# Adding the gated results to the token tiles by accumulating transfers of GpSimd instead of VectorE

## The chip, the core and the metric

The kernel runs on one core of a Trainium2 chip. A core has five engines that run side by side and meet at semaphores: TensorE (PE) multiplies matrices into eight banks of PSUM, VectorE (DVE) and ScalarE (ACT) work on tiles in SBUF and PSUM, GpSimd (POOL) computes in SBUF and issues transfers, and SyncE (SP) issues transfers. The transfers of all of them are carried out by the core's 16 DMA engines. The metric is the time of one execution on the device in microseconds (us); before the change it is 453.1 us, the median of three runs (452.22 to 453.49).

## The reference

The input x has 32 sequences of 128 tokens with 512 features in float32. Cut to what matters, each sequence goes through two residual halves:

```python
m = mask[:, :, None]
shift, scale, gate_msa = jnp.split(silu(t) @ ada_w + ada_b, 3, axis=1)
norm = jnp.where(m, layernorm(x) * (1 + scale[:, None]) + shift[:, None], 0.0)
ssm_out = jnp.where(m, mlp_fwd(norm) + mlp_bwd(norm), 0.0)   # exact gelu
x = x + gate_msa[:, None] * ssm_out
shift, scale, gate_mlp = jnp.split(silu(t) @ ffada_w + ffada_b, 3, axis=1)
ff_norm = layernorm(x) * (1 + scale[:, None]) + shift[:, None]
h = gelu(ff_norm @ ff_w1 + ff_b1, approximate=True)          # 512 -> 1024
return x + gate_mlp[:, None] * (h @ ff_w2 + ff_b2)           # 1024 -> 512
```

The first half counts only where the mask is set, which is a small part of the tokens. The second half is done for all 4096 tokens and is most of the work. The last line, `x + gate * result`, is what the change touches.

## The kernel before, in words

The opening (about the first 68 us) gathers the masked tokens into 512 slots, runs the first half on them, and leaves their new rows in a DRAM tensor, `x1_rows`. The rest is a loop over four **pairs**. A pair is two **sides** of four sequences each, so 1024 tokens; its tokens lie in four tiles x of 128 x 2 x 512, two for each side. Eight such tiles exist in the pool, so two pairs' tokens are in SBUF at a time, and the tokens of the pair after the next can only be loaded into a tile once its finished tokens have been stored.

Both matrix products of a pair are done by a scheme with seven block products in place of eight (P1 to P7), the first one nested twice. The **first product** (`FirstProduct`) works in streams 1, 2, 5, 6, 3, 7, 4; each stream has two banks, called e and a, and seven phases. Streams 5, 6, 7 and 4 read weight sums `tw` that are loaded from DRAM (`load_weights`, line 1069). Between the phases other engines alter the banks: `seed` (DVE, line 1167), the sum after P6 (DVE, line 1148, which needs a sum that POOL makes at line 1174), the sums after P7 and P4 (DVE, lines 1153 and 1158). PE then goes on in the same bank.

The **second product** (`SecondProduct`) runs over two column halves U and V in the order P1U P5U P1V P5V P2U P6U P2V P6V P3U P7U P3V P7V P4U P4V. Whenever a quarter of the output is complete in its bank, `finish` multiplies it by the gate into a tile t of 128 x 512 (line 1284; four buffers) and adds t to one half of the features of a token tile x (line 1286). There are eight such finishes in a pair. When both halves of a token tile are done, `store` (line 1290) sends the tile to the output, 512 KB, from SP's queue. While the second product of a pair runs, the tokens of the next pair are normalised, turned by small SBUF transfers into xT (line 961), scaled (ACT, line 944) and summed (DVE, line 991), and the first streams of its first product are put between the last steps (P4U and P4V).

All order is written out by hand: each engine gets its instructions in the order of the program, and every queue is in order. On SP's queue, at the end of a pair, there stand in a row the stores of the first two token tiles, the weights tw of stream 5, the loads of two token tiles of the pair after the next (line 412), the stores of the other two tiles, the weights tw of stream 6, and the loads of the last two tiles. On POOL's queue, after the sums of a first product, there stand the two gate loads of 1 MB each (line 901), and then the sums of the next first product (line 1174), mixed with gathers (line 890) that overwrite the rows of masked tokens in the newly loaded token tiles; a gather waits for the load of its tile. The last pair loads no tokens and gathers none.

Of the kernel before, what the change touches and what calls it, by code (L numbers as in the profile page):

```python
# [14 lines left out]
ALU = mybir.AluOpType  # L15
# [7 lines left out]
def kernel(  # L23
# [49 lines left out]
    nc = tc.nc  # L73
# [4 lines left out]
    NP = B // (2 * G)  # L78
# [99 lines left out]
    def group_of_tiles(name):  # L178
        return xnp.tile([P, G, D], F32, tag="xn", name=f"xn_{name}")
# [35 lines left out]
    def project(i, h, w, name, between=None, bank=(ps_o, "o"), seeded=None):  # L215

        pool, tag = bank
        po = seeded or pool.tile([P, 512], F32, tag=tag, name=f"po_{name}_{i}")
        for f in range(HC):
            if between and f in between:  # L220
                between[f]()
            nc.tensor.matmul(  # L222
                po,
                h[f][:, ts(i, P)],
                w[:, f, :],
                start=(f == 0 and seeded is None),
                stop=(f == HC - 1),
                skip_group_check=seeded is not None,
            )
        return po  # L230
# [6 lines left out]
    def gated(po, bias, gate, name):  # L237

        t = tp.tile([P, D], F32, tag="t", name=f"t_{name}")
        nc.vector.tensor_tensor(t, po, bias, ALU.add)  # L240
        nc.vector.tensor_tensor(t, t, gate, ALU.mult)
        return t
# [476 lines left out]
    def in_blocks(t):  # L719
        return t.rearrange("p g (h f) -> p (g h) f", f=2 * P)  # L720
# [59 lines left out]
    for f in range(KC):  # L780
        hidden_of_tile(f, 1)
        for done in (f - 1, f) if f % 2 else ():
            t = ssm.tile([P, NH], F32, tag="h", name=f"h_s0_{done}", bufs=HC)
# [28 lines left out]
    t = in_blocks(group_of_tiles("tw_3"))  # L812
# [418 lines left out]
    class SecondProduct:  # L1231
# [46 lines left out]
        def finish(self, c, side, h, result):  # L1278

            part = slice(h * D // 2, (h + 1) * D // 2)  # L1280
            view = result.rearrange("p (i d) -> p i d", i=2)
            t = tp.tile([P, 2, D // 2], F32, tag="t", name=f"t_o{self.p}_{c}_{side}{h}")
            gate = self.gate[side][:, 2 * c : 2 * c + 2, part]
            nc.vector.tensor_tensor(t, view, gate, ALU.mult)
            xt = self.xs[side][c][:, :, part]
            nc.vector.tensor_tensor(xt, xt, t, ALU.add)

        def store(self, c, side):
            b = (2 * self.p + side) * G + 2 * c
# [299 lines left out]
    with tc.If(more > 0):  # L1589
# [11 lines left out]
        with tc.For_i(0, more, 1):  # L1601
# [12 lines left out]
            for half_no, (mod, was, wbs, bias, bcol, func) in enumerate(  # L1614
# [25 lines left out]
                t = gated(project(0, h_l, wb, f"l{half_no}"), bias, gate_l, f"l{half_no}")  # L1640
# [59 lines left out]
```

## Time and profile before

| | before |
|---|---|
| median of three runs | 453.1 us (452.22 to 453.49) |
| profiled execution, span from the first to the last instruction | 451.7 us |
| part of the median that lies outside this span | 1.4 us |
| PE busy | 444.0 us (98%) |
| DVE busy | 334.5 us (74%) |
| ACT busy | 177.9 us (39%) |
| POOL busy | 158.4 us (35%) |
| granted TensorE clock | 1.000 |
| bytes moved by transfers | 70.84 MB, mean 157 GB/s |

The profiled execution is known by its span; the time of a run is longer by what lies around the span. Busy times are sums over one execution. Rows of a timeline give the start of an instruction from the beginning of the span, its duration, the engine, the line of the kernel, what it writes and reads, and in brackets the idle time of the engine before it with what ended that idle time. A queue's own rows carry a q (SPq, POOLq). An issue of a transfer is over long before the transfer has landed; landing times are in a list of their own.

### The profile page before, as it was taken

The page shows a single profiled execution, that of the slowest core. Times are in us where ns is not written, and L with a number is a line of the kernel's source. Part 1 is how long each engine was busy: PE and PEld are TensorE (multiplying, and loading weights), DVE is VectorE, ACT ScalarE, POOL GpSimd, SP SyncE. Part 2 cuts the span into 40 slices and gives each one's busy share as a digit, 9 for nine tenths or more (in the row PEclk, how much of TensorE's full clock was granted, in tenths as well). Part 3 has the DMA queues.
Part 4 walks back from the last instruction along what each step waited for, and adds up shares of the span by engine and source line. Part 5 has one row for each costly group of instructions (what it writes and reads, how often), then busy time and mean ns, then how long its engine had stood idle before and what let it go on. Part 6 is the DMA issues. An engine that isn't in the chain of part 4 may idle for free.

```text
span 451.7 us, 6204 instructions
## 1 busy us (share of the span) xinstructions
PE 444.0 (98%) x2147; PEld 370.2 (82%) x2147; DVE 334.5 (74%) x573; ACT 177.9 (39%) x389; POOL 158.4 (35%) x154
## 2 busy tenths in 40 slices
PE   8999999999999999999999999999999999999995
PEld 3884675688888888888888888888888888888884
DVE  5797788877799759977895689878956885434645
ACT  3123116353651551536526415464265244642000
POOL 4211470089770000897600007977000027560000
PEclk9999999999999999999999999999999999999999
DMA  6999449857327717741396177512971534122022
GB/s 250 372 399 408 177 65 308 284 187 229 129 97 168 108 49 268 235 138 36 105 177 93 46 267 230 141 38 86 189 99 47 176 128 129 35 93 95 0 94 96
DMA packets 85440, 70.84 MB, mean 157 GB/s; under 512 B 63396, under 2 KB 64508, under 8 KB 84382
## 3 DMA queue, kind: packets, MB, share of 16 engines
q1 hardware_dynamic: 64270, 57.76, 42.3%
q0 software_dynamic: 4160, 10.54, 6.9%
q10 hardware_dynamic: 16976, 2.11, 3.9%
q8 instruction: 18, 0.29, 0.3%
q14 instruction: 16, 0.13, 0.1%
HBM read 56.71 MB, written 13.70 MB: 156 GB/s over the span
## 4 chain that ended last, share of the span: by engine, by line
PE 84%; DMA 8%; DVE 3%; issue 2%; POOL 1%; SPq 0%; POOLq 0%
PE a_o L1310 24%; PE a_m L1123 21%; PE e_o L1310 18%; PE e_m L1123 16%; DMA fw<-in_L_cond_ff_w_dram 3%; PE po_s L222 3%; DMA w<-in_L_cond_bwd_w_dram 3%; DMA x_wide<-t_s 2%; DMA x<-x_wide,slot_i 1%; DVE t L403 1%; PE last L1310 1%; PE a_m_alone L1123 1%; POOL x L819 1%; PE ptr L950 0%; PE pl_s L255 0%
## 5 line engine op out<-in xcount | busy, mean ns | idle before, releaser
L1174 POOL TENSOR_TENSOR ha<-p_m,ha 128x512 f32<-128x512 f32 x20 | 25.8, 1292 | 176.0 <-ACT ha L1181 166.1
L1310 PE MATMUL e_o<-fw,ha 128*128 128x256 f32 x256 | 57.9, 379 | 0.0
L944 ACT ACTIVATE xT<-xT,modT 128x128 f32<-128x128 f32 x112 | 44.0, 480 | 28.1 <-DMA xT<-xn 28.1
L1310 PE MATMUL a_o<-t,hb 128*128 128x256 f32 x240 | 54.1, 379 | 0.0
L1310 PEld LDWEIGHTS e_o<-fw,ha 128*128 128x128 f32 x256 | 48.6, 190 | 6.6
L1310 PEld LDWEIGHTS a_o<-t,hb 128*128 128x128 f32 x240 | 45.6, 190 | 6.2
L1085 ACT ACTIVATE hb<-hb,biasT 128x256 f32<-128x256 f32 x64 | 29.0, 500 | 28.3 <-POOL hb L1207 16.1
L1137 ACT COPY p_m<-e_m 128x512 f32<-128x512 f32 x27 | 15.8, 586 | 51.6 <-PE e_m L1123 51.6
L890 POOL DMA_INDIRECT x<-x_rows,slot_i x24 | 27.2, 1135 | 6.2 <-issue 5.4
L1174 POOL TENSOR_TENSOR hb<-p_m,hb 128x512 f32<-128x512 f32 x20 | 29.2, 1460 | 0.3
L1310 PE MATMUL a_o<-fw,ha 128*128 128x256 f32 x128 | 28.9, 379 | 0.0
L1310 PE MATMUL a_o<-t,s 128*128 128x256 f32 x128 | 28.9, 379 | 0.0
L1310 PE MATMUL e_o<-fw,s 128*128 128x256 f32 x128 | 28.9, 379 | 0.0
L222 PE MATMUL po_s<-w,h_s 128*128 128x512 f32 x64 | 28.4, 594 | 0.0
L1181 ACT COPY ha<-e_m 128x512 f32<-128x512 f32 x32 | 18.5, 579 | 24.8 <-PE e_m L1123 24.4
L1310 PEld LDWEIGHTS a_o<-fw,ha 128*128 128x128 f32 x128 | 24.3, 190 | 3.3
L1310 PEld LDWEIGHTS a_o<-t,s 128*128 128x128 f32 x128 | 24.3, 190 | 3.3
L1310 PEld LDWEIGHTS e_o<-fw,s 128*128 128x128 f32 x128 | 24.3, 190 | 3.3
L1148 DVE TENSOR_TENSOR e_m<-a_m,ha 128x512 f32<-128x512 f32 x20 | 14.0, 698 | 17.0 <-POOL ha L1174 7.6
L1085 ACT ACTIVATE ha<-e_m,biasT 128x256 f32<-128x256 f32 x48 | 20.0, 468 | 14.4 <-PE e_m L1123 14.4
L1123 PE MATMUL a_m<-xT,tw 128*128 128x256 f32 x96 | 24.7, 380 | 0.0
L1123 PE MATMUL e_m<-s,fw 128*128 128x256 f32 x92 | 23.7, 380 | 0.0
(234 smaller groups left out, 894.1 us busy)
## 6 DMA issues: line engine op xcount, KB each, us to landing
x<-in_x_dram SPq DMA_DIRECT2D x16, 512.0 KB, 5.9
tw<-t_rows SPq DMA_DIRECT2D x16, 512.0 KB, 4.3
gate<-gate_rows POOLq DMA_DIRECT2D x8, 1024.0 KB, 5.1
out_dram<-x SPq DMA_DIRECT2D x15, 512.0 KB, 4.7
tw<-t_rows SPq DMA_DIRECT2D x16, 384.0 KB, 3.9
xT<-xn SPq DMA_DIRECT2D x80, 64.0 KB, 2.7
ada_f<-in_L_cond_ffada_w_dram SPq DMA_DIRECT2D x4, 768.0 KB, 14.8
ada_a<-in_L_cond_ada_w_dram SPq DMA_DIRECT2D x4, 512.0 KB, 3.6
```

Of the source, the lines that this page charges most:

```text
L222: nc.tensor.matmul(po, h[f][:, ts(i, P)], w[:, f, :], start=(f == 0 and seeded is None), stop=(f == HC - 1), skip_group_check=seeded is no ...
L403: engine.tensor_tensor(out, x, y, ALU.subtract)
L819: nc.gpsimd.indirect_dma_start(out=raw[i // 2][:, i % 2], out_offset=None, in_=x1_wide[:slots], in_offset=bass.IndirectOffsetOnAxis(ap=slo ...
L890: nc.gpsimd.indirect_dma_start(out=xs[i // G][i % G // 2][:, i % 2], out_offset=None, in_=x1_rows, in_offset=bass.IndirectOffsetOnAxis(ap= ...
L944: nc.scalar.activation(out, src, AF.Identity, bias=shift, scale=scale)
L1085: nc.scalar.activation(dst[:, n], src[:, n], AF.Gelu_apprx_tanh, bias=biasT[:, f : f + 1])
L1123: nc.tensor.matmul(bank[:, ts(n, QT)], self.w_block(j, product)[:, ts(n, P)], self.x_block(j, product), start=(product in ("P1", "P5") and ...
L1137: nc.scalar.copy(p5, e)
L1148: nc.vector.tensor_tensor(e, a, p5, add)
L1174: nc.gpsimd.tensor_tensor(self.place(RESULT[j], c), self.p5[j], other, ALU.add)
L1181: nc.scalar.copy(self.place(RESULT[j], c), src)
L1310: nc.tensor.matmul(part, src[:, k, ts(i, P)], w[product][:, k, :], start=(last and k == 0), stop=True, skip_group_check=True,)
```

## The change

In the first three pairs the addition at line 1286 is no longer an instruction of DVE. GpSimd issues a transfer from t to the same half of the token tile x, from SBUF to SBUF, that adds what it brings to what lies there; a partition's row of 512 values goes into two pieces of 256 values. The last pair keeps the addition on DVE. Everything else stays as written.

```diff
             gate = self.gate[side][:, 2 * c : 2 * c + 2, part]
             nc.vector.tensor_tensor(t, view, gate, ALU.mult)
             xt = self.xs[side][c][:, :, part]
-            nc.vector.tensor_tensor(xt, xt, t, ALU.add)
+            if self.p + 1 < NP:
+                nc.gpsimd.dma_start(xt, t, accum_op=ALU.add)
+            else:
+                nc.vector.tensor_tensor(xt, xt, t, ALU.add)
```

24 rows leave DVE and 24 come to POOL; line numbers behind the change grow by three. On POOL, at the end of the first pair, between the gate loads and the first sums of the second pair's first product (x_205 to x_208 are the four token tiles of the pair, t_o_0 and t_o_1 the gated results of U and V):

```order
 L901 DMA gate_0_1193<-gate_rows 128x2048
 L901 DMA gate_1_1237<-gate_rows 128x2048
+L1287 DMA x_205<-t_o_0_00_1303 128x2x256
+L1287 DMA x_206<-t_o_1_00_1358 128x2x256
+L1287 DMA x_205<-t_o_0_01_1389 128x2x256
+L1287 DMA x_207<-t_o_0_11_1414 128x2x256
+L1287 DMA x_206<-t_o_1_01_1427 128x2x256
+L1287 DMA x_208<-t_o_1_11_1447 128x2x256
+L1287 DMA x_207<-t_o_0_10_1474 128x2x256
+L1287 DMA x_208<-t_o_1_10_1494 128x2x256
 L1174 TENSOR_TENSOR ha_1432<-p_m_2_1514,ha_1432 128x2x256
 L1174 TENSOR_TENSOR hb_1433<-p_m_2_1514,hb_1433 128x2x256
```

Where POOL had nothing between the gate loads and the next pair's sums, eight issues now stand in the order of DVE's multiplications, and each waits for its own.

On DVE, the last finishes of the first pair (s, xT and sx are the blocks of the next pair's tokens):

```order
 L1284 TENSOR_TENSOR t_o_1_01_1427<-e_o_1_1212,gate_0_1193 128x512
-L1286 TENSOR_TENSOR x_206<-x_206,t_o_1_01_1427 128x2x256
 L991 TENSOR_TENSOR s_1_1402<-xT_0_1248,s_1_1401 128x1024
-L1340 TENSOR_TENSOR c_o_1_1445<-a_o_1_1213,p_o_1_1287 128x512
+L1343 TENSOR_TENSOR c_o_1_1445<-a_o_1_1213,p_o_1_1287 128x512
 L1284 TENSOR_TENSOR t_o_1_11_1447<-c_o_1_1445,gate_1_1237 128x512
-L1286 TENSOR_TENSOR x_208<-x_208,t_o_1_11_1447 128x2x256
 L1051 TENSOR_TENSOR sx_1459<-s_1_1401 128x512
 L1051 TENSOR_TENSOR sx_1459<-xT_0_1248 128x512
 L1284 TENSOR_TENSOR t_o_0_10_1474<-a_o_0_1155,gate_1_1237 128x512
-L1286 TENSOR_TENSOR x_207<-x_207,t_o_0_10_1474 128x2x256
 L1051 TENSOR_TENSOR sx_1459<-xT_1_1315 128x512
```

The additions are gone, and what stood behind them has moved up; the multiplications stay where they were.

On SP the rows and their order are the same, and only what the stores wait for is new. The last store of the first pair and the rows behind it, before:

```order
L1290 DMA out_dram<-x_208 128x2x512 [waits DMASW3_49,DMAHW4_49,DMASW2_49,DVE_49]
L1069 DMA tw_1_1498<-t_rows 128x1024 [waits DMASW1_49]
L1069 DMA tw_1_1498<-t_rows 128x768
L412 DMA x_1501<-in_x_dram 128x2x512 [waits DMAHW7_49,DMAHW3_49]
L412 DMA x_1503<-in_x_dram 128x2x512 [waits DMAHW4_49,DMAHW0_49]
```

and now:

```order
L1293 DMA out_dram<-x_208 128x2x512 [waits DMAHW4_49,DMASW7_49,DMASW1_49]
L1069 DMA tw_1_1498<-t_rows 128x1024 [waits DVE_49]
L1069 DMA tw_1_1498<-t_rows 128x768
L412 DMA x_1501<-in_x_dram 128x2x512 [waits DMAHW7_49,DMAHW3_49]
L412 DMA x_1503<-in_x_dram 128x2x512 [waits DMAHW4_49,DMAHW0_49]
```

The store waited for DVE's addition; it now waits for transfers that GpSimd issued (the DMASW semaphores). The wait for DVE has moved to the weights behind it, whose buffer is the one that DVE's multiplications read the gate from. The weights and the token loads still stand behind it.

## The prediction

> **What bounds the kernel now.** I read the page first: engine shares and the chain of waits.
>
> ```profile
> PE 444.0 (98%) x2147; PEld 370.2 (82%) x2147; DVE 334.5 (74%) x573; ACT 177.9 (39%) x389; POOL 158.4 (35%) x154
> PE 84%; DMA 8%; DVE 3%; issue 2%; POOL 1%; SPq 0%; POOLq 0%
> ```
>
> TensorE (PE) is busy for 444.0 of 451.7 us. Whether the rest lies where the change acts is told by the busy times by stretch, cut at the three places where one pair gives way to the next (columns: PE, weight loads, DVE, ACT, POOL, granted clock, DMA share, GB/s).
>
> ```profile
> 0.00:68.00 68.00, 65.04 (x423) 44.67 (x424) 52.25 (x144) 17.39 (x38) 25.37 (x44) 1.00 0.79 278
> 159.00:250.00 91.00, 91.00 (x422) 79.55 (x421) 71.28 (x108) 43.19 (x97) 36.07 (x30) 1.00 0.53 137
> 250.00:341.00 91.00, 91.00 (x422) 79.57 (x421) 71.37 (x108) 41.07 (x92) 36.06 (x30) 1.00 0.54 136
> ```
>
> From 159 to 341 us PE has no idle time at a full clock, and the waits of the opening are over before the first changed instruction (145 us). What PE still loses shows only in the chain, as a group of eight matmuls that takes longer than the usual 1.73:
>
> ```profile
> 199.53 0.86 PE e_m L1123 x4
> 200.39 1.97 PE a_m L1123 x8
> 202.36 0.86 PE e_m L1123 x4
> ```
>
> That is 0.24 us per pair. So relief for VectorE (DVE) has next to nothing to win; the question is which waits the change brings near PE.
>
> **What it removes.** The groups of DVE:
>
> ```profile
> L1286 DVE TENSOR_TENSOR x<-x,t_o 128x512 f32<-128x512 f32 x32 | 22.2, 692 | 1.1
> ```
>
> 24 of the 32 go, 24 x 0.692 = 16.6 us of DVE. All of it lies under matmuls, so I book 0 us. The cover is PE's own work, and it stays.
>
> **What it adds on GpSimd (POOL).** Eight transfers of 256 KB per pair stand in POOL's queue behind the two gate loads and ahead of the first sum of the next pair. POOL's timeline:
>
> ```profile
> 133.34 0.55 POOL L901 DMA_DIRECT2D gate<-gate_rows  x1 [1.45 <-PE a_m L1123]
> 181.22 1.26 POOL L1174 TENSOR_TENSOR ha<-p_m,ha 128x512 f32<-128x512 f32 x1 [47.34 <-ACT ha L1181]
> 190.06 1.23 POOL L890 DMA_INDIRECT x<-x_rows,slot_i  x1 [0.30 <-issue]
> 191.60 1.50 POOL L890 DMA_INDIRECT x<-x_rows,slot_i  x1 [0.30 <-ACT p_m L1137]
> 193.12 1.28 POOL L1174 TENSOR_TENSOR ha<-p_m,ha 128x512 f32<-128x512 f32 x1
> ```
>
> POOL is idle for 47.34 us just where they stand. No accumulating transfer is in the trace, so its issue is bounded by 0.55 us (gate, 128 rows) and 1.50 us (slowest gather); two pieces per partition make me take 1.1 us. The first seven end long before 181.22. The eighth waits for the last multiplication of DVE:
>
> ```profile
> 164.16 1.23 DVE L991 TENSOR_TENSOR s<-xT 128x1024 f32<-128x1024 f32 x1 [5.50 <-ACT xT L944]
> 169.63 0.68 DVE L1284 TENSOR_TENSOR t_o<-e_o,gate 128x512 f32<-128x512 f32 x1
> 178.21 0.68 DVE L1284 TENSOR_TENSOR t_o<-a_o,gate 128x512 f32<-128x512 f32 x1
> 178.93 0.69 DVE L1286 TENSOR_TENSOR x<-x,t_o 128x512 f32<-128x512 f32 x1
> ```
>
> The multiplication ends at 178.21 + 0.68 = 178.89; its issue is through at 180.0, 180.4 at the most, before 181.22. POOL pays nothing there: 0 us.
>
> **What it delays.** The store of a token tile now waits for the landing of a transfer in place of an addition of 0.69 us. Let L be the time from the end of the multiplication to the landing. Behind the stores on SP's queue, in order, stand the next weights (tw) and the tokens of the pair after (x):
>
> ```profile
> 171.07 0.38 SPq L1290 DMA_DIRECT2D out_dram<-x  x1
> 176.79 3.25 SPq L1290 DMA_DIRECT2D out_dram<-x  x2
> 180.09 1.34 SPq L1069 DMA_DIRECT2D tw<-t_rows  x2
> 181.52 1.95 SPq L412 DMA_DIRECT2D x<-in_x_dram  x2
> ```
>
> The last store goes at 176.79 + 3.25 - 0.38 = 179.66, 0.77 after 178.89. So it, and everything behind it, moves by D = L - 0.77. What that meets, by the landing times of the issue list (last column) and of the gathers:
>
> ```profile
> gate<-gate_rows POOLq DMA_DIRECT2D x8, 1024.0 KB, 5.1
> x<-in_x_dram SPq DMA_DIRECT2D x16, 512.0 KB, 5.9
> tw<-t_rows SPq DMA_DIRECT2D x16, 512.0 KB, 4.3
> ...
> DMA to landing us min/median/max: 2.5/3.1/5.4
> ```
>
> and by the readers, on PE and DVE:
>
> ```profile
> 167.41 1.03 PE L1123 MATMUL e_m<-s,fw 128*128 128x256 f32 x4
> 189.85 1.03 PE L1123 MATMUL e_m<-xn_sy,tw 128*128 128x256 f32 x4
> 197.64 1.03 PE L1123 MATMUL e_m<-xn_sy,tw 128*128 128x256 f32 x4
> 196.10 0.70 DVE L1148 TENSOR_TENSOR e_m<-a_m,ha 128x512 f32<-128x512 f32 x1
> ```
>
> Weights: issued at 180.09, landed at 184.39, read by PE at 189.85. They bear D = 5.46, so L = 6.2 us.
>
> Gathers: the x load issued at 181.52 lands at 187.42; the gather that writes into its tile is POOL's at 190.06, which leaves 2.64. If that gather waits, the sum L1174 behind it, which ends at 193.12 + 1.28 = 194.40, is late. DVE's L1148 needs it and must end by 197.64, where PE reads the bank: 197.64 - 0.70 - 194.40 = 2.54 more. Together D = 5.18, so L = 5.9 us. This case exists at two of the three places, since the third has no pair left to load. There only the weights count:
>
> ```profile
> 361.31 0.39 SPq L1290 DMA_DIRECT2D out_dram<-x  x1
> 361.80 0.41 SPq L1069 DMA_DIRECT2D tw<-t_rows  x1
> 371.75 1.03 PE L1123 MATMUL e_m<-xn_sy,tw 128*128 128x256 f32 x4
> ```
>
> 361.80 + 4.3 = 366.10 against 371.75: D = 5.65, L = 6.4 us. I take the second place as equal to the first.
>
> **How long is L?** Through GpSimd's queue a gather lands in 3.1 us and the gate's 1024 KB in 5.1. In between, 256 KB come to 3.1 + 2.0 x 256/1024 = 3.6 us on a quiet chip. The rings are not quiet where the last four of a pair run:
>
> ```profile
> 139.00:157.00 18.00, 18.00 (x85) 15.86 (x84) 15.59 (x21) 7.43 (x18) 0.00 (x0) 1.00 0.80 111
> 171.00:187.00 16.00, 16.00 (x76) 14.05 (x75) 15.21 (x23) 4.74 (x10) 5.30 (x4) 1.00 0.94 321
> ```
>
> From 171 to 187 us they are busy for 0.94 of the time. Gathers range up to 5.4, 2.3 over their median; I add half of that, 1.1, so L = 4.7 us. Bounds: not under the shortest gather, 2.5; not over the gate's 1024 KB plus the 2.3 of a crowded ring plus a second 0.55 of issue for the doubled pieces, 8.0. I stay near the low end since the bytes are a quarter of the gate's. At 4.7, 5.9 is not reached and nothing is paid.
>
> One rule speaks against the change. The Trainium skill (Collectives: The Full Stack, The bandwidth ceiling) says that an add in a transfer needs two source reads, which halved the measured bandwidth. By it the 256 KB would count as 512 and L would be an estimated 5.2 instead of 4.7; the sum would be the same, with less to spare. No run so far shows it.
>
> The four buffers of t are now freed by the landing, no longer by DVE's addition, so DVE's multiplications wait for transfers. The tile written at 169.63 comes round again some 8 us later, at 178.21; an L below that holds nobody up. Above it the next phase's sums for PE's banks, which stand behind on DVE, would be late.
>
> **Sum.** 0 (DVE) + 0 (POOL's issues) + 0 (stores, weights and gathers within their slack), and 0.2 us for POOL and DVE sharing the stretch after 181 us in another alignment, the size of the one stall seen. The profiled span is 451.7 us; the median of the runs, 453.1, lies 1.4 above it, which I carry along. Forecast: 453.3 us, no change. What a measurement here can tell from no change is about 0.3%, 1.4 us.
>
> **Rivals.**
>
> *Late landings make it slower.* From L = 5.9 us on, gather and sum on POOL, and a little later the weights, reach PE. For it: 0.94 DMA share, an unknown operation, two in-order queues behind it. Against it: rows of transfers with four times the bytes land in 5.1. At L = 8.0: (8.0 - 5.9) x 2 + (8.0 - 6.4) = 5.8 us, so 459 us. Over 1.4 us needs L above 6.4. Chance 0.33.
>
> *The turned blocks are held up.* From 139 to 157 us the small xT pieces keep the rings busy for 0.80; 18 x 0.20 = 3.6 us are free. Two transfers fall into it. At 321 GB/s one takes 0.8 us, with both operands read 1.6, both together 3.3 us: hidden. DVE's L991 ends at 164.16 + 1.23 = 165.39 and PE reads its result at 167.41, 2.0 us of slack. It would need twice that price, 6.6: 6.6 - 3.6 - 2.0 = 1.0 us at three places, 456 us. Chance 0.08.
>
> *DVE's relief shows.* Without the additions the 0.24 us at each of three places may go, and as much again elsewhere in a pair: 3 x 0.48 = 1.4 us, 451.7 us. Against it: PE shows no other gap. Chance 0.05. A smaller gain is part of the forecast.
>
> **How the numbers follow.** No change 0.54, the two slower cases 0.33 + 0.08 = 0.41, faster 0.05; the same three numbers are the chances of within 0.3%, slower and faster. The forecast's own range is 452.2 to 454.5. The range for 8 in 10 takes in L up to the bound with a little of both slower cases together: 452.0 to 460.0.
>
> **What would show it.** Right: PE still without idle time from 159 to 341 us; the store at 179.66 moves by some 4 us; the gather at 190.06 moves by less than 2.6 us; 24 fewer rows at the addition's line. Wrong: a PE group ended by DMA tw at about 190 us or by DVE L1148 at about 198 us, or gaps near 167 us behind ACT's scaling of xT. A landing of an accumulating transfer over 6 us would break the forecast; under 4 us it would make every slower case void.

## The result and the profile after

The changed kernel takes 470.2 us (median of four runs, 469.72 to 471.59) beside 452.7 us for the kernel before (four runs here, 452.22 to 453.49): 1.0385 times as long, 95% interval 1.0363 to 1.0407. No change was forecast, with 460.0 us as the upper end of the range. Its profiled execution took 469.7 us with a span of 468.0, 16.3 us more than the span of before. In all that follows one execution counts as slow, 470.8 us of a kernel whose other three took 458.3 to 463.9; it is left out of that kernel's ratio, and its trace is not used.

The busy times of the page, and the two stretches between pairs that were free of idle PE time before (columns as in the prediction: PE, weight loads, DVE, ACT, POOL, granted clock, DMA share, GB/s):

```profile
PE 451.3 (96%) x2147; PEld 374.5 (80%) x2147; DVE 318.5 (68%) x549; ACT 178.0 (38%) x389; POOL 185.9 (40%) x178
```

```profile
159.00:250.00 91.00, 86.38 (x384) 74.42 (x383) 62.34 (x96) 38.06 (x83) 43.50 (x37) 0.96 0.62 151
250.00:341.00 91.00, 85.90 (x385) 74.49 (x385) 61.18 (x96) 38.05 (x83) 43.57 (x37) 0.96 0.62 149
```

DVE is 16.0 us lighter, near the 16.6 that the prediction booked, and POOL heavier by 27.5. PE, which had no idle time here, now lacks 4.6 and 5.1 us in the two stretches, and its clock is no longer whole. PE's timeline at the end of the first pair and of the second says where (in brackets the idle time before and what ended it):

```profile
168.26 1.13 PE L1123 MATMUL e_m<-s,fw 128*128 128x256 f32 x4 [0.81 <-DVE s L991]
...
194.66 2.04 PE L1123 MATMUL e_m<-xn_sy,tw 128*128 128x256 f32 x4 [3.69 <-DMA tw<-t_rows]
196.50 1.91 PE L1123 MATMUL a_m<-xn_sy,tw 128*128 128x256 f32 x4
198.21 1.91 PE L1123 MATMUL e_m<-sx,tw 128*128 128x256 f32 x4
199.92 1.50 PE L1123 MATMUL a_m<-sx,tw 128*128 128x256 f32 x4
201.25 1.03 PE L1123 MATMUL e_m<-xn_sy,tw 128*128 128x256 f32 x4
...
294.16 2.05 PE L1123 MATMUL e_m<-xn_sy,tw 128*128 128x256 f32 x4 [5.10 <-DMA tw<-t_rows]
```

Three losses stand in these rows. PE waits 3.69 and 5.10 us for the next weights. Behind each wait, four groups that take 1.03 us elsewhere take 1.25 to 2.05: 3.2 us more in the first place, 3.0 in the second (2.05, 1.91, 1.91 and 1.25). And about 0.9 us goes to the turned blocks at 168 us. Together 8 us in the first place and 8 in the second; the third loses 0.2. That is the whole 16.3.

Why the weights are late is told by the chain of waits at the second place:

```profile
277.00 0.70 DVE t_o L1284
277.71 0.28 issue
277.99 10.42 DMA x<-t_o
...
288.46 0.38 SPq L1293
288.85 0.05 issue
288.90 5.12 DMA tw<-t_rows
```

The last multiplication of the pair ends at 277.70; the transfer that adds its result lands at 288.41 (277.99 + 10.42); only then go the store and the weights behind it on SP's queue. With L as in the prediction, the time from the end of the multiplication to the landing, L is 10.7 us here. At the first place the multiplication, POOL's issue, SP's last store and the weights are these:

```profile
178.93 0.69 DVE L1284 TENSOR_TENSOR t_o<-a_o,gate 128x512 f32<-128x512 f32 x1 [0.71 <-PE a_o L1313]
179.92 1.18 POOL L1287 DMA_DIRECT2D x<-t_o  x1 [1.77 <-DVE t_o L1284]
189.07 0.38 SPq L1293 DMA_DIRECT2D out_dram<-x  x1
189.51 0.46 SPq L1069 DMA_DIRECT2D tw<-t_rows  x1
```

L = 189.07 - 179.62 = 9.4 us, where 4.7 were forecast and 8.0 was the upper bound. At the third place, where no tokens are loaded, the same rows give 6.2 us.

How full the transfer engines are goes with it. The stretches from multiplication to landing of the third, the fifth and the last transfer of the first pair (the column before the last is the DMA share):

```profile
157.82:162.29 4.47, 4.47 (x22) 3.95 (x21) 0.00 (x1) 1.60 (x5) 1.17 (x1) 1.00 0.73 113
172.41:176.41 4.00, 4.00 (x21) 3.51 (x20) 3.96 (x6) 0.59 (x1) 2.34 (x2) 1.00 0.63 96
179.62:189.07 9.45, 9.45 (x45) 8.30 (x44) 7.30 (x11) 4.60 (x9) 4.12 (x3) 1.00 1.08 304
```

With a share of 0.73 and 0.63 a transfer lands in 4.5 and 4.0 us; with a share of 1.08 (over 1, since packets overlap) it takes 9.4.

The DMA queue of GpSimd, before and then after (packets, MB, share of 16 engines over the span):

```profile
q0 software_dynamic: 4160, 10.54, 6.9%
```

```profile
q0 software_dynamic: 10688, 16.84, 15.5%
```

0.155 x 468.0 - 0.069 x 451.7 = 41.4 us of all 16 engines for 24 transfers: 1.7 us each. This is the time of their packets, which can overlap; it is called their ring time below. The added packets are (10688 - 4160) / 24 = 272 for each transfer.

### The profile page after: what moved, and what is told of

Read it like the earlier page. It is cut to its first block, busy times and chain, and to the rows that moved or that the text cites. A ratio compares the mean times of both kernels' runs of the same rounds, so it can differ in the third digit from the quotient of the medians.

```text
span 468.0 us, 6242 instructions
## 1 busy us (share of the span) xinstructions
PE 451.3 (96%) x2147; PEld 374.5 (80%) x2147; DVE 318.5 (68%) x549; ACT 178.0 (38%) x389; POOL 185.9 (40%) x178
## 3 DMA queue, kind: packets, MB, share of 16 engines
q0 software_dynamic: 10688, 16.84, 15.5%
## 4 chain that ended last, share of the span: by engine, by line
PE 68%; DMA 14%; DVE 6%; SPq 4%; issue 3%; ACT 2%; POOL 2%; POOLq 0%; ACTq 0%; DVEq 0%
PE a_o L1313 18%; PE a_m L1123 17%; PE e_m L1123 14%; PE e_o L1313 13%; SPq L961 3%; DMA fw<-in_L_cond_ff_w_dram 3%; PE po_s L222 3%; DMA w<-in_L_cond_bwd_w_dram 2%; DMA x<-t_o 2%; DMA tw<-t_rows 2%; DMA x_wide<-t_s 2%; ACT xT L944 1%; DMA xT<-xn 1%; DMA x<-x_wide,slot_i 1%; DVE t L403 1%
## 5 line engine op out<-in xcount | busy, mean ns | idle before, releaser
L1287 POOL DMA_DIRECT2D x<-t_o x24 | 28.4, 1184 | 111.4 <-DVE t_o L1284 102.6
L1167 DVE TENSOR_TENSOR e_m<-a_m,ha 128x512 f32<-128x512 f32 x20 | 14.0, 699 | 26.6 <-PE a_m L1123 26.4
L1148 DVE TENSOR_TENSOR e_m<-a_m,ha 128x512 f32<-128x512 f32 x20 | 13.9, 698 | 17.0 <-POOL ha L1174 7.6
```

The lines of the kernel that those rows point to most:

```text
L1167: nc.vector.tensor_tensor(e, a, self.place(PRIOR[j], "11"), ALU.add)
L1287: nc.gpsimd.dma_start(xt, t, accum_op=ALU.add)
```

## The experiments

The theory after this reading: the last transfers of a pair land late because each takes 1.7 us of rings that are already full (the queues of the 16 engines), and what stands behind them on SP's queue, first the weights, then the tokens, reaches PE late; the half clock follows from PE's standing idle. The rivals: that the early transfers do it through the turned blocks, that POOL's issues do it, or that the clock falls for another reason. Times are medians beside runs of the kernel before on the same chip (452.9 for the first four, 453.3 for the next four, 452.8 for the last four).

**Half of the transfers.** Only the four additions of side 0 of each pair stay transfers:

```diff
-            if self.p + 1 < NP:
+            if self.p + 1 < NP and side == 0:
```

> Only the four transfers of side 0 stay per pair (the first, second, third and fifth); the additions of side 1 are back on VectorE. Theory 'the last landings of a pair come late' (crowded rings, two in-order queues behind them, then a slow clock): the side-1 stores wait for VectorE again and the weights go out in time, so about 454.5 us (453 to 456), with no PE wait on weights near 190 us. Rival 'every accumulating transfer costs its share' (traffic, VectorE waiting for buffers): half of the 17.4 us stays, about 461 us.

Measured: 460.1 us, ratio 1.0168 (1.0142 to 1.0194), close to the rival's time. Its trace has no half clock. PE stands 0.7 us for the turned blocks and twice 1.61 us for DVE's L1153, 3.9 of the 5.9 us by which its span is longer; the rest was not found. GpSimd's sums and DVE's rows ahead of the first of these:

```profile
196.22 1.27 POOL L1174 TENSOR_TENSOR ha<-p_m,ha 128x512 f32<-128x512 f32 x1
...
201.15 1.28 POOL L1174 TENSOR_TENSOR ha<-p_m,ha 128x512 f32<-128x512 f32 x1
202.38 1.27 POOL L1174 TENSOR_TENSOR hb<-p_m,hb 128x512 f32<-128x512 f32 x1
```

```profile
201.51 2.17 DVE L927 TENSOR_SCALAR ve<-mv 128x4 f32<-128x4 f32 x1
203.60 0.68 DVE L1153 TENSOR_TENSOR hb<-a_m,hb 128x512 f32<-128x512 f32 x1
```

The row of L927 in the kernel before:

```profile
199.48 1.10 DVE L927 TENSOR_SCALAR ve<-mv 128x4 f32<-128x4 f32 x1
```

The sum at 196.22 stood at 193.12 before: the gather ahead of it waited for a late token load. DVE's tiny L927 now falls beside GpSimd's sums and holds DVE for 2.17, and L1153 stands behind it. So even early transfers delay the token loads, and their lateness is enlarged behind them.

**The last two alone.**

```diff
-            if self.p + 1 < NP:
+            if self.p + 1 < NP and side == 1 and h == 0:
```

> Only the last two transfers of each pair stay (P4, side 1); six additions are back on VectorE. Theory 'rings crowded because the earlier transfers push the stores, weights and token loads into the last ones': without the earlier ones the second store, the first weights and the first token loads leave at about 171 to 175 us as before, the last landing takes 5 to 6 us and its store goes by 185 us, within the slack of about 6: 453.5 us (452.5 to 456). Rival 'the last landing is slow by itself': the landing still takes 9 us, PE waits for weights and drops its clock at two places, 462 us or more.

Measured: 457.8 us, ratio 1.0113 (1.0090 to 1.0135), between the two. The last multiplication of the first pair and SP's last two stores:

```profile
176.82 0.69 DVE L1284 TENSOR_TENSOR t_o<-a_o,gate 128x512 f32<-128x512 f32 x1 [1.20 <-PE a_o L1313]
179.62 2.28 SPq L1293 DMA_DIRECT2D out_dram<-x  x2
```

The last store goes at 179.62 + 2.28 - 0.38 = 181.52: with only two transfers per pair the last one lands 4.0 us after its multiplication, not 9.4, and PE does not wait for weights. What is left are waits of 0.50 and 1.57 us for L1153. So the landing is no property of the transfer by itself: it is late where the six others run ahead of it. This was read from the fastest of the four executions, 454.7 us; the others took 457.2 to 458.7, and what they lost is in no trace.

**The same transfers as plain copies.** This kernel leaves the adding of the gated results to x out and copies them over x instead:

```diff
-                nc.gpsimd.dma_start(xt, t, accum_op=ALU.add)
+                nc.gpsimd.dma_start(xt, t)
```

> All 24 transfers stay but copy instead of adding (the sum with x is left out, so the output lacks the residual). The transfers of the changed kernel take 8.6% of 16 engines' span, 1.7 us each; a copy of the same pieces should take about half. If that doubled ring time makes the landings late: the last landing comes about 2 us earlier, about 465 us. If the landings are late by standing behind other traffic, whatever they carry: 469 to 470 us. If the adding itself were all of it: 453 us.

Measured: 458.0 us, ratio 1.0117 (1.0096 to 1.0137), far below the changed kernel. L falls to 6.2 us and 4.3 at the first two places, and the wait for weights to 0.78 us and nothing; there is no half clock. Two waits of 1.59 and 1.27 us for L1153 remain. Its q0 row reads 10.7% of 456.2 us: (48.8 - 31.2) / 24 = 0.73 us of the rings for a copy, against 1.7 for an addition. The issue on POOL is 0.72 us against 1.17. The same bytes, queues and waits are there, so 12 of the 17 us come from what an adding transfer costs beyond a copy. That need not be the adding alone. The row of the copies' queue:

```profile
q0 software_dynamic: 6080, 16.84, 10.7%
```

A copy goes in (6080 - 4160) / 24 = 80 packets, an adding transfer in 272, so its pieces are smaller as well. No run here separates the two. The shares of the busiest stretch, of the kernel before, the plain copies and the changed kernel:

```profile
178.00:190.00 12.00, 12.00 (x57) 10.54 (x56) 10.78 (x17) 5.97 (x12) 7.45 (x6) 1.00 0.87 306
```

```profile
178.00:190.00 12.00, 11.49 (x54) 9.73 (x52) 9.85 (x16) 5.98 (x12) 8.17 (x7) 1.00 0.95 338
```

```profile
178.00:190.00 12.00, 12.00 (x58) 10.52 (x57) 9.14 (x14) 5.38 (x11) 5.09 (x5) 1.00 1.06 300
```

The changed kernel's rings are full (a share over 1 counts packets that overlap) and move fewer bytes per second than the copies. The Trainium skill (Collectives: The Full Stack, The bandwidth ceiling) says that an add needs two source reads and so halved the bandwidth of a reduction there; the ring time here, 1.7 against 0.73 us, agrees in size, but the smaller packets may have a part in it.

**Weights ahead of the last stores** on SP's queue:

```diff
                 self.finish(c, 1, 0, a)
-                self.store(c, 1)
+                if p + 1 == NP:
+                    self.store(c, 1)
...
             put(13, lambda: nxt["p"].load_weights(2))
+            for c in range(2):
+                put(13, second.store, c, 1)
```

> All 24 accumulating transfers stay; on SP's queue the weights of stream 6 now stand ahead of the two stores of side 1, not behind them. Theory 'the gathers and the sum behind them are the next wait': PE no longer waits for weights near 190 us, but near 198 us for VectorE's sum, which waits for POOL's sum behind a gather that waits for a token load; about 3 us and the slow clock again at two places, about 466 us (463 to 469). Rival 'the weights are the whole price': about 455 us.

Measured: 468.3 us, ratio 1.0338 (1.0321 to 1.0356), as expected. PE no longer waits for weights at the first place (1.48 us at the second), and stands a little later:

```profile
202.19 2.07 PE L1123 MATMUL e_m<-xn_sy,tw 128*128 128x256 f32 x4 [3.49 <-DVE e_m L1148]
```

This is the prediction's second path, gather and sum to DVE's L1148, as it was written. In the changed kernel it was hidden behind the wait for the weights; taken alone it costs nearly as much.

**The gathers behind the sums as well.** On top of the last edit, two gathers of side 1 go to POOL after the sums:

```diff
-            put(2, 6, take_first_half, p + 1, x_next, range(G, G + 2 + (p == 0)))
-            if p:
-                put(3, 4, take_first_half, p + 1, x_next, range(G + 2, G + 3))
+            if p == 0:
+                put(2, 6, take_first_half, p + 1, x_next, range(G, G + 3))
+            else:
+                put(3, 4, take_first_half, p + 1, x_next, range(G, G + 3))
```

> As the run with the weights ahead of the stores (468.3 us), and the two gathers that wait for the late token load now stand on POOL behind the sum L1174 of stream 6, not ahead of it. Theory 'late weights, and behind them the late gather in front of the sum, are nearly the whole price': no PE wait on L1148 near 198 us, a clock of 1.0 throughout, 458 us (455 to 461; what is left: 0.9 us of the turned blocks, about 1.5 us of weights at the second place, some 1.6 us at each place behind L1153). Rival 'there is a third wait of the same size' (for instance VectorE's statistics waiting for the gathers): 464 us or more.

Measured: 462.9 us, ratio 1.0183 (1.0125 to 1.0240), runs of 458.3, 461.9 and 463.9 us beside the one of 470.8, whose trace is not used. The median lies between the two expectations. By it the path over the gathers was worth some 5 us; with runs so far apart and no trace the size is rough, and that the wait for L1148 is gone is not shown.

**Two small waits undone.** The last-two kernel, with the stats root that holds L927 later in every pair:

```diff
-            put(*((4, 1) if p else (5, 4)), stats[0].root)
+            put(5, 4, stats[0].root)
```

> As the run with only the last two transfers (457.8 us), and the small instruction of VectorE at L927 (128x4, 2.16 us there, 1.1 us before the change, 0.14 us at best) stands later, as it does in the first pair. Theory 'VectorE's L927 is held while POOL's sums run, and with POOL's row of sums shifted by a microsecond this falls on PE's bank at L1153': without it the two waits of about 0.5 and 1.6 us on L1153 go, 455.5 us (454 to 456.5). Rival 'PE waits because POOL's sums themselves are late': no change, 457 to 458.5 us.

Measured: 455.7 us, ratio 1.0069 (1.0045 to 1.0093), as expected. The waits for L1153 are gone; 0.36 and 0.34 us remain at two others. It is the fastest of the kernels with transfers in all three pairs, and slower than the kernel before. The gain is one of the medians; the two profiled executions, each the fastest of its four, have spans of 452.9 us here and 452.7 with L927 in its old place.

**Work for PE where it waited.** Twenty matmuls that nobody reads, just ahead of the product that needs the new weights, in the second and third pair; then the same with ten:

```diff
+        if p in (1, 2):
+            pf = ps_t.tile([P, 512], F32, tag="tr", name=f"pf_{p}")
+
+            def filler(n=20):
+                for _ in range(n):
+                    nc.tensor.matmul(pf[:, :2 * P], ident, fw1[:, 0, :2 * P], start=True, stop=True)
+
+            put(2, 6, filler)
```

> The changed kernel with 20 matmuls of 128x256 (0.216 us each, 4.3 us) that nobody reads, put on PE just ahead of the block that waits for the weights, in the second and third pair. Theory 'after the wait PE runs at half clock for 6.8 us because it stood idle': the filler uses up the wait (3.7 and 5.1 us) without an idle stretch of that length, the clock stays 1.0, and 3 us are saved at each of two places, less 0.5 where the filler is longer than the wait: about 464.6 us (463.5 to 466). Rival 'the clock goes down for another reason than the idle stretch': 470 us, or more by what the filler adds.

> The filler of 20 matmuls took 8.8 us of TensorE, twice what was meant; ten take 4.3 us (8.65 / 2). They cover the wait of 3.69 us in the second pair and all but 0.8 us of the 5.10 us in the third. If the half clock comes from TensorE's standing idle, it stays away at both places, and the time is 453 + 2 x 4.3 + 0.8 + 1.0 (the first pair) = 463.4 us (461.5 to 465). If the clock falls for another reason of the change, some 3 us more are lost at each place and it stays at 469 to 471 us. A stall at the turned blocks in the first pair, if it shows, adds up to 6 us to either.

Measured: 474.4 us (471.7 to 477.0), ratio 1.0450 (1.0393 to 1.0506), with twenty; 472.8 us (472.0 to 473.5), ratio 1.0433 (1.0417 to 1.0449), with ten. By their times both missed. A matmul of this kind is two rows in the trace, so twenty take 8.7 us, twice what was meant, and two of these fillers alone cost 17 us. The short one is readable. Its first place and its second (at 293 us):

```profile
195.06 4.48 PE L1507 MATMUL pf<-fw,ident 128*128 128x256 f32 x20
200.08 1.10 PE L1123 MATMUL e_m<-xn_sy,tw 128*128 128x256 f32 x4 [0.55 <-DMA tw<-t_rows]
201.02 1.03 PE L1123 MATMUL a_m<-xn_sy,tw 128*128 128x256 f32 x4
```

```profile
293.18 4.48 PE L1507 MATMUL pf<-fw,ident 128*128 128x256 f32 x20
297.50 1.03 PE L1123 MATMUL e_m<-xn_sy,tw 128*128 128x256 f32 x4
```

The waits of 3.69 and 5.10 us are covered and the groups behind take 1.03 us: with PE busy the half clock stays away. That part was as expected. The time was not, for other reasons: at 170.8 us PE stood 3.25 us for the turned blocks (with half clock behind it, some 5 us together), and twice 1.60 us for L1153. Adding 8.7 + 5.1 + 3.4 and 2 us of small waits to 451 gives 470; its span is 471.8.

**Token loads last** on SP's queue, behind stores and weights:

```diff
-                put(11, lambda: x_of[p + 2][0].extend(load_side(p + 2, 0)))
...
+                put(13, lambda: x_of[p + 2][0].extend(load_side(p + 2, 0)))
                 put(13, lambda: x_of[p + 2][1].extend(load_side(p + 2, 1)))
```

> All 24 accumulating transfers; on SP's queue all four token loads of the pair after the next now stand behind the last stores and weights, so nothing but one store and one pair of weights is in the rings when the last two transfers run. Theory 'the last landing takes 9.4 us because it stands behind the token loads and weights in the rings': the last store goes within 6.5 us of VectorE's last multiplication, PE waits less than 1 us for the weights near 191 us, and then for the gathers, which are later still (so the time tells little, 460 to 475). Rival 'the accumulating transfer is slow by itself': the last store is still 8 us or more behind the multiplication.

One execution: 477.9 us. The last transfers landed 4.5, 7.6 and 6.6 us after their multiplications (185.57 to 190.09, 283.21 to 290.77, 384.15 to 390.77), against 9.4, 10.7 and 6.2 in the changed kernel. So a part of the late landing at the first two places seems to be the megabyte of tokens that goes out between the transfers, and the third place, which has none, is unmoved. At the first place another thing changed as well: PE stood 3.80 us for the turned blocks, and the last multiplication came 5.2 us behind the one before it, not 2.9. The kernel with the long filler has the same spacing with the tokens in their old place, and there L is 7.1 us; against that the tokens are worth 2.6. It is no cure: the tokens come later, and PE waits 4.27 and 4.31 us for DVE's L1153 in place of the weights.

**The changed kernel again**, unchanged, beside the last three:

> The changed kernel once more, unchanged, as the measure for the three kernels beside it. If what was read of its one trace is all, it takes 470.2 us (469 to 472), with one wait of 0.8 us for the turned blocks in the first pair. If the turned blocks' stall of 3.3 to 3.8 us, which three other kernels with all 24 transfers showed, belongs to the change and comes and goes, some executions take 474 to 478 us.

Measured: 471.9 us (468.7 to 472.6), ratio 1.0397 (1.0366 to 1.0427), as the first time. L is 9.4, 10.7 and 7.3 us; PE waits 0.77 us for the turned blocks, 3.30 and 5.23 us for weights, 0.85 at the third place, and in this execution also 1.60 and 1.08 us for L1153, behind an L927 of 2.16 and 2.17 us. So the 3.3 us for the turned blocks in the short filler's kernel, which ran beside it on the same chip, is no matter of the chip; what decides between 0.8 and 3.3 us was not found.

**The last five alone.** The first three additions of a pair, those that run beside the turning of blocks, go back to DVE:

```diff
-            if self.p + 1 < NP:
+            if self.p + 1 < NP and (side == 1 or (h == 1 and c == 1)):
```

> The first three additions of each pair are on VectorE again, the last five stay transfers. Theory: only the early transfers hold up the turned blocks and only the late ones hold up the weights. Then TensorE waits 0.3 us or less for the turned blocks of the first pair, still 3.7 and 5.1 us for the weights with the half clock behind each, and the time is 469.2 us (468 to 470.5), the same in every execution. Rival: the early transfers push work into the crowded stretch too, and without them the waits on the weights shrink to 1 to 2 us without the half clock: 457 to 461 us.

Measured: 464.7 us (462.4 to 465.3), ratio 1.0245 (1.0221 to 1.0269), between the two. ACT's last turned blocks, of before, of the changed kernel and of this one:

```profile
157.87 6.26 ACT L944 ACTIVATE xT<-xT,modT 128x128 f32<-128x128 f32 x16 [2.36 <-DMA xT<-xn]
```

```profile
160.69 6.27 ACT L944 ACTIVATE xT<-xT,modT 128x128 f32<-128x128 f32 x16 [4.00 <-DMA xT<-xn]
```

```profile
157.13 6.26 ACT L944 ACTIVATE xT<-xT,modT 128x128 f32<-128x128 f32 x16 [2.34 <-DMA xT<-xn]
```

Without the early transfers the blocks come as before and PE does not wait there: the early ones do hold them up. PE still waits 2.84 and 3.49 us for weights with the half clock behind it, so the late ones alone make the main stall; but these waits are shorter than the 3.30 and 5.23 us beside them, and L is 8.2 and 7.7 us. The theory that the two act apart was too strict: by these times the early three account for 7 of the 19 us.

**The third pair alone.**

```diff
-            if self.p + 1 < NP:
+            if self.p + 2 == NP:
```

> Only the third pair's eight additions are transfers; behind it no token tiles are loaded. In the changed kernel that pair's last transfer landed 6.2 us after its multiplication and cost TensorE 0.2 us. Theory: a landing of 6.2 us is within what the weights bear, so the time is 453.3 us (452.8 to 454.0), no change. Rival: transfers add small waits wherever they are used, as 1.6 us for VectorE's copies behind GpSimd's sums: 454.5 to 456 us.

Measured: 454.2 us (453.3 to 455.2), ratio 1.0027 (1.0015 to 1.0040): 1.2 us slower, a little above the theory's range and below the rival's. The multiplication, the last store and PE's reader of the weights:

```profile
359.03 0.69 DVE L1284 TENSOR_TENSOR t_o<-a_o,gate 128x512 f32<-128x512 f32 x1 [1.35 <-PE a_o L1313]
```

```profile
365.22 1.61 SPq L1293 DMA_DIRECT2D out_dram<-x  x2
```

```profile
371.57 1.10 PE L1123 MATMUL e_m<-xn_sy,tw 128*128 128x256 f32 x4 [0.49 <-DMA tw<-t_rows]
```

The store goes at 365.22 + 1.61 - 0.39 = 366.4, so L = 6.7 us, and PE waits 0.49. Eight transfers where no tokens are loaded cost about a microsecond, and win nothing.

## Why the prediction was wrong

**The relief of DVE is worth nothing: right.** DVE has 16.0 us less to do and no kernel here is faster than before. The buffers of t held nobody up either: in the trace of after no multiplication waits for a transfer.

**POOL's eight issues cost nothing: right.** The issue takes 1.17 us, 1.1 were taken; the eighth ends at 179.92 + 1.18 = 181.10, and the first sum behind it, at 182.2, waits for ACT.

**Store, weights and tokens move by L - 0.77, and the weights bear 6.2 us (6.4 at the third place): right.** At the third place L and the wait go together: 6.2 us and a loss of 0.2, 6.7 and 0.49 (the third pair alone), 7.3 and 0.85 (the changed kernel again). At the second place L - 6.2 = 4.5; the weights' own landing, 5.12 us in place of the 4.3 of the list, makes it 5.3; measured 5.10. At the first place 3.2 + 0.7 (landing 5.02) less the 0.9 that PE was late itself is 3.0; measured 3.69. The second path, to DVE's L1148, was there as written, and showed as soon as the weights went first.

**L = 4.7 us, 3.6 on a quiet chip and 1.1 for crowded rings: this step failed, in its second term.** The quiet part was near: the third and the fifth transfer of the first pair land in 4.5 and 4.0 us. The crowded part of the last one was not 1.1 but 5.8 and 7.1 at the first two places (9.4 and 10.7 less 3.6) and 2.6 at the third. It was priced from how far single gathers stray, as if the new transfers met a crowd, when they make much of it: with the first six gone the last one lands in 4.0 us, and with copies in their place, 0.73 us of the rings for each in place of 1.7, in 6.2 and 4.3.

The prediction had numbers that pointed there. For the other rival it priced an adding transfer at 1.6 us of the rings (1.7 measured), and it read that from 171 to 187 us they are busy for 0.94. Five transfers run there, 5 x 1.7 = 8.5 us of work against 0.06 x 16 = 1.0 us of free time; 7.5 us must go late, and 3.6 + 7.5 = 11.1 is near the 10.7 of the second place. This sum is made after the fact, and it is too high elsewhere: it gives 11.1 us for the last five alone, where L is 8.2 and 7.7, 6.0 for the last two alone, where it is 4.0, and 6.3 for the copies, where it is 6.2 and 4.3. So it is an upper estimate; how the late work shares itself out is not shown. The upper bound of 8.0 failed by the same: a bound from rows of single transfers does not hold for a queue of them.

**Rival "Late landings make it slower": right in its mechanism, too small in its price.** At its L of 8.0 it gave 459 us. (By its own rule 1.4 us are reached at L = 6.5, not 6.4.) With the measured 9.4, 10.7 and 6.2 its rule, (L - 5.9) at the first two places and (L - 6.4) at the third, gives 8.3 us, which is about the 8.8 us that PE stands for weights. That is partly luck: its 5.9 us are those of the path over the gathers, which shows only once the weights go first, and the weights bear 6.2 but take 5.0 and 5.1 us to land, not 4.3. The other half of the 17 us was in no step.

**The 0.2 us for POOL and DVE in another alignment: too small where it shows.** In the first trace of the changed kernel there is no such wait; in the second PE waits 1.60 and 1.08 us for L1153.

**What was in no step: the clock.** Behind each long wait the granted clock is half. The changed kernel, in the stretches of the wait, right behind it, a little later, and after that (the column before the last two is the clock):

```profile
190.97:194.66 3.69, 0.01 (x1) 0.03 (x1) 2.49 (x5) 0.00 (x0) 2.95 (x3) 0.92 0.97 292
194.66:197.86 3.20, 3.19 (x8) 2.57 (x9) 0.00 (x0) 1.11 (x3) 0.67 (x1) 0.50 0.95 345
198.06:201.26 3.20, 3.20 (x10) 2.52 (x10) 1.47 (x3) 0.66 (x2) 2.09 (x3) 0.56 0.23 42
201.66:204.66 3.00, 3.00 (x15) 2.64 (x15) 2.67 (x6) 1.17 (x2) 3.00 (x3) 1.00 0.42 163
```

Half clock for over 6 us costs 3 us, nearly as much as the wait did. The trace of before has no wait of PE over 1.12 us after its first 60 us, so nothing in it showed this; the prediction priced waits at their own length and did not ask what follows one.

**Rival "The turned blocks are held up": half right.** PE stood 0.8 us for them at the first place of the changed kernel and not at the other two, and the last-five kernel shows that the early transfers cause it. In three of the kernels with all 24 transfers the same wait was 3.3 to 3.8 us.

**"DVE's relief shows": wrong**, with no trace of a gain.

## What to carry to other kernels

Price a transfer that joins full rings by the ring time it adds, all of them together against the free share of that stretch, and not by how single transfers stray. At the first two places of the kernels above that sum came out between near and 3.4 us too high, so it serves as the upper end of a range. An adding transfer took 2.3 times the ring time of a copy here (1.7 against 0.73 us), smaller packets included. Then follow the in-order queue behind what waits for its landing: here a store that comes 10 us late took the weights with it. And a wait of the matmul engine that passes some 2 to 3 us should be booked with up to 3 us more, for the clock behind it: it was half for 3.41 or 6.83 us behind every wait here from 2.84 us on.

## What was not expected of the hardware

An adding transfer of 256 KB within SBUF, in pieces of 1 KB, held POOL 1.17 us for its issue (0.72 without the addition), landed 4.0 to 4.5 us after its operand was ready where the rings had room (a share of 0.63 and 0.73), and took 1.7 us of all 16 engines in 272 packets; the same transfer without the addition took 0.73 us in 80.

The granted clock. After the first 60 us, the traces of before, after and eleven experiments hold 39 waits of PE of 0.7 us or more. After each of the 26 from 0.72 to 1.66 us the clock stayed at 1.00; after each of the 13 from 2.84 to 5.23 us it read 0.50 to 0.67 over the next 3.2 us. Either side of the step, the wait and what follows, the first from the kernel with the token loads last and the second from the last five alone:

```profile
294.56:296.22 1.66, 0.01 (x1) 0.03 (x1) 1.66 (x4) 0.00 (x0) 0.00 (x0) 1.00 0.98 297
296.22:299.42 3.20, 3.20 (x15) 2.84 (x16) 1.53 (x3) 1.72 (x4) 0.00 (x0) 1.00 1.02 385
```

```profile
189.31:192.15 2.84, 0.00 (x1) 0.03 (x1) 2.48 (x5) 0.00 (x0) 0.63 (x1) 0.97 0.92 311
192.15:195.35 3.20, 3.20 (x8) 2.58 (x9) 0.00 (x0) 1.12 (x3) 0.00 (x0) 0.50 0.90 330
195.55:198.75 3.20, 3.20 (x16) 2.83 (x15) 2.74 (x5) 1.06 (x3) 2.26 (x3) 1.00 0.39 109
```

The Trainium skill (TensorE: Matmul & The Clock Gate, What's actually happening) says that the clock falls to half after an idle window of about 3.4 us and comes back after a busy one. The traces agree on the half and on the length, 3.41 or 6.83 us, one or two such windows; here 2.84 us of idle time were already enough, and the measurement decides.

A DVE instruction on 128x4 values (L927) took 1.10 us in the trace of before and 2.17 us where it began beside the first of two sums of GpSimd. In the kernel with the last two transfers alone PE's wait of 1.57 us behind it went when L927 stood later; the kernel with half of the transfers and the changed kernel's second trace have the same rows, and there it was not tried.

Open stays how much of an adding transfer's price is the adding and how much its smaller packets, why the turned blocks were late by 0.8 us in some kernels and by 3.3 to 3.8 in others of the same order up to that place, and 1 to 2 us of the time of the filler kernels.
